# Graph kernel with two attention layers on one core: layer 0's logit projections as four row strips instead of narrow columns, and a smaller, split load ahead of them

## The chip, the cores and the metric

The kernel runs on one core of one Trainium2 chip. The metric is device time in microseconds (us), the median of several executions. TensorE (PE) multiplies matrices, and its weight loads are listed apart as PEld; VectorE (DVE), ScalarE (ACT) and GpSimd (POOL) do the rest; SyncE (SP), ScalarE and GpSimd issue the DMAs. Each engine takes its own instructions in the order in which the program gives them.

## The reference, cut to what matters

`x` is 2708 x 256 and `adj` is 2708 x 2708, nearly all of it zeros. Two layers follow one another, each with a residual and a row-wise norm:

```python
# layer 0, three heads; adj without its diagonal is A
for W, a in heads:                       # W: 256 x 256, a: 512 x 1
    hW = x @ W
    hp = (A > 0) @ hW
    hm = (A < 0) @ hW                    # zero here: no entry of adj is negative
    e  = leaky_relu(concat([hp, hm], axis=1) @ a)
    # softmax over the neighbours with logits e[j], times A, times hW; mean over the heads
out0 = diag(adj) * (gru_edge(A @ x, x) + gru_node(mean_of_heads, x))
x = layernorm(x + out0)
# layer 1: a four-head graph attention on the mask adj > 0.5, residual, layernorm
```

Because `hm` is zero, `e` is `(A > 0) @ (x @ (W @ a[:256]))`. So each head needs one vector `W @ a[:256]` of 256 numbers, and then one number for each row of x. For three heads these numbers are called `u`, 2708 x 3. Only the first 256 of the 512 entries of each `a` enter.

## The kernel before, in words

The rows are cut into 22 blocks of 128 (the last has 20), and the columns into six groups: five of 512 (four blocks each) and one of 148.

The first phase passes over the transposed adjacency group by group, two row blocks at a time. For each pair of blocks, SP loads 128 x 2 x 512 floats (512 KB) into one of five buffers. ACT turns them into 0/1 masks with two Sign passes (into rings of three, `over` and `mask`). DVE takes a maximum over stretches of 64 columns (`found0`). PE then adds the masks up in four matmuls, each on its own 32 columns of the array, that is, on its own 32 rows of a PSUM bank (`only`, `only`, and `u3` twice). The weights `u3` of the last two are the numbers `u` of these row blocks, split into three bf16 parts.

During the first group, each four blocks also load a part of x transposed (`xT`, 256 x 512) and compute their `u` with `projected_u`. It takes three steps:

- `uw`, the three vectors `W @ a[:256]`, is made once by DVE, in six products with a sum along the row (`scalar_tensor_tensor` with `accum_out`). It needs all of `gat_w` (768 KB) and of `a_b` (`a` on all partitions, 768 KB), which ACT's queue loads with one DMA each.
- For each row block, and for both halves of the 256 features, a matmul takes 128 columns of `xT` as weights and streams the three columns of `uw` through them.
- DVE copies the 128 x 12 results out of PSUM and splits them into three bf16 parts (`split3`).

PE has further work without a due time there: 60 `keep` products (the GRU's terms in x for five groups), whose results ACT and DVE copy out of PSUM by turns and SP writes to DRAM.

When the maxima of a group are complete, `listed` and `spread` make lists of the rows that have entries in each stretch of columns. From these lists POOL gathers adjacency rows and table rows with indirect DMAs. The second phase multiplies them for layer 0 and runs the two GRU cells by group; the third does the same for layer 1.

No order is written by hand. Every instruction is noted first (class `Plan`), with a cost from a small model: a float32 matmul costs at least 0.22 or 0.26 us, a transpose 0.11, a DMA 2.5 us and its size at 250 GB/s. A list scheduler then issues, on each engine, the ready instruction with the longest tail behind it. Matmuls into one bank that are noted in a row are issued as one. So each cost that changes can change the order of everything after it. All notes carry line 219 of the profile, where the scheduler calls them, and lines are therefore told apart by the names of tiles. `f_home` stands for several tiles that share one allocation (`uw`, `u3`, `f_u`, the masks and three of the five adjacency buffers among them); the other two buffers are `f_edge_wi` and `f_node_wi`. `side` is a ring of two PSUM banks.

Of the kernel before, what the change touches and what calls it, by code (L numbers as in the profile page):

```python
# [10 lines left out]
F32 = mybir.dt.float32  # L11
# [9 lines left out]
P = 128  # L21
D = 256
KD = D // P
HEADS0 = 3
# [6 lines left out]
CH = 512  # L31
# [277 lines left out]
def fast_path(ctx: ExitStack, tc: tile.TileContext, i: dict, out: bass.AP, bad: bass.AP):  # L309
# [11 lines left out]
    nc = plan = Plan(tc.nc)  # L321
# [6 lines left out]
    GR = CH // P  # L328
    groups = [list(range(g, min(g + GR, NB))) for g in range(0, NB, GR)]
    NG = len(groups)  # L330
    base = [g[0] * P for g in groups]
    width = [sum(size[c] for c in g) for g in groups]
# [20 lines left out]
    def ring(tiles):  # L353

        return cycle(tiles).__next__
# [4 lines left out]
    def banks(name, n):  # L360
        return [ps.tile([P, CH], F32, name=f"{name}{k}") for k in range(n)]
# [3 lines left out]
    side, pl_bank, ls_bank = ring(banks("side", 2)), ring(banks("pl", 1)), ring(banks("ls", 1))  # L365
# [19 lines left out]
    ident = const.tile([P, P], F32, name="f_ident")  # L385
# [32 lines left out]
    QUARTER = P // 4  # L418
# [33 lines left out]
    for t, of in ((less_room, TILES0 + TILES1), (less_whole, WHOLE0 + WHOLE1)):  # L452
        c = 0
        while c < len(of):
            e = c
# [3 lines left out]
            c = e  # L459
# [41 lines left out]
    def on_every(src, wide):  # L501
        return bass.AP(tensor=src.tensor, offset=src.offset, ap=[[0, P], [1, wide]])

    def row_bcast(pool, src, wide, name, queue):
        t = pool.tile([P, wide], F32, name=name)
        queue.dma_start(t, on_every(src, wide))
        return t


    def split3(pool, parts, v, p, n, name):  # L510

        rest = pool.tile([P, n], F32, name=name)[:p]
        if len(v.shape) == 3:
            rest = rest.rearrange("p (b h) -> p b h", h=v.shape[2])
        nc.vector.tensor_copy(parts[0], v)
        nc.vector.tensor_sub(rest, v, parts[0])
        nc.vector.tensor_copy(parts[1], rest)
        nc.vector.tensor_sub(rest, rest, parts[1])
        nc.vector.tensor_copy(parts[2], rest)

    xT = const.tile([P, KD, N], F32, name="f_xT")
# [6 lines left out]
    gat_w = const.tile([P, HEADS0, KD, D], F32, name="f_gat_w")  # L528
# [172 lines left out]
    ap, tiles = Rings(const, 1, home2), Rings(const, 8, home1)  # L701
# [1 line left out]
    nc.vector.memset(u3, 0.0)  # L703
    e_col = const.tile([P, NB, HEADS0], F32, name="f_e_col")
    nc.gpsimd.memset(e_col, 0.0)
    nc.scalar.dma_start(gat_w, i["L0_gnn_gat_W"].rearrange("h (k p) e -> p h k e", p=P))
    a_b = row_bcast(ap, i["L0_gnn_gat_a"], HEADS0 * 2 * D, "f_a_b", nc.scalar)

    uw = ap.tile([P, KD, HEADS0], F32, name="f_uw")
    junk = ap.tile([P, D], F32, name="f_junk")  # L710
    for h in range(HEADS0):
        for k in range(KD):
            nc.vector.scalar_tensor_tensor(
                junk, gat_w[:, h, k, :], 1.0, a_b[:, 2 * h * D : (2 * h + 1) * D],
                op0=ALU.mult, op1=ALU.mult, accum_out=uw[:, k, h : h + 1],
            )

# [4 lines left out]
    def projected_u(g):  # L722
        bl = groups[g]
        n = len(bl) * HEADS0
        pu = side()
        for m, b in enumerate(bl):
            for k in range(KD):
                nc.tensor.matmul(
                    pu[: size[b], m * HEADS0 : (m + 1) * HEADS0], lhsT=xT[:, k, b * P : b * P + size[b]],
                    rhs=uw[:, k, :], start=(k == 0), stop=(k == KD - 1),  # L730
                )
        u = ap.tile([P, GR * HEADS0], F32, name="f_u", bufs=2)
        full = sum(size[b] == P for b in bl) * HEADS0
        if full:
            nc.vector.tensor_copy(u[:, :full], pu[:, :full])
        if full < n:
            nc.vector.memset(u[:, full:n], 0.0)
            nc.vector.tensor_copy(u[: size[last], full:n], pu[: size[last], full:n])
        split3(
            ap, [u3[:, bl[0] : bl[-1] + 1, s * HEADS0 : (s + 1) * HEADS0] for s in range(3)],  # L740
            u[:, :n].rearrange("p (b h) -> p b h", h=HEADS0), P, n, f"f_u_rest{len(bl)}",
        )
# [31 lines left out]
    for b in range(0, NB, 7):  # L774
        e = min((b + 7) * P, N)
# [106 lines left out]
    for g, cs in enumerate(groups):  # L882
        w = width[g]
        sums_of = (accs[0], dbs[0])[g % 2]
        c0, nf = base[g] // W0, w // W0
        for b0 in range(0, NB, 2):
# [4 lines left out]
            for b in pair:  # L891
                if g == 0 and b % GR == 0:
                    load_xT(b // GR)
                    projected_u(b // GR)
# [17 lines left out]
            for b in pair:  # L912
                if b in cs:
                    p, o = size[b], b * P - base[g]
                    v = at2[:p, b - b0, o : o + p]
# [16 lines left out]
            for q, (lhs, rhs) in enumerate(  # L932
# [3 lines left out]
                p = size[pair[q % 2]]  # L936
                nc.tensor.matmul(
                    sums_of[q * QUARTER : (q + 1) * QUARTER, :w], lhsT=lhs[:p], rhs=rhs[:p],
                    start=(b0 == 0), stop=(b0 + 2 == NB),
# [358 lines left out]
    for h in range(HEADS1):  # L1298
        for k in range(KD):
            nc.tensor.matmul(  # L1300
                pm[:C1, h : h + 1], lhsT=w1[:, k, h * C1 : (h + 1) * C1], rhs=xmean[:, k : k + 1],
                start=(k == 0), stop=(k == KD - 1), skip_group_check=True,
# [124 lines left out]
def tile_adj_resnorm(tc: tile.TileContext, i: dict, out: bass.AP):  # L1427
    nc = tc.nc
    with tc.tile_pool(name="guard", bufs=1) as gp:
        bad = gp.tile([P, 1], F32, name="bad")  # L1430
        fast_path(tc, i, out, bad)
        with tc.tile_pool(name="guard_ps", bufs=1, space=PSUM) as ps:
            one = gp.tile([P, 1], F32, name="guard_ones")
            nc.vector.memset(one, 1.0)
            nc.vector.tensor_scalar(bad, bad, 0.0, None, op0=ALU.is_gt)
            n = ps.tile([1, 1], F32, name="n_bad")
            nc.tensor.matmul(n, lhsT=bad, rhs=one, start=True, stop=True)
            flag = gp.tile([1, 1], I32, name="flag")
            nc.vector.tensor_copy(flag, n)
        taken = nc.values_load(flag[0:1, 0:1], min_val=0, max_val=P)  # L1440
        with tc.If(taken > 0):
            general_path(tc, i, out)
# [436 lines left out]
```

## Time and profile before

| | |
|---|---|
| median of 3 runs | 847.95 us (843.71 to 849.48) |
| the profiled execution | 842.26 us, its span 840.3 us |
| PE busy | 732.8 us, 87% of the span |
| DVE / ACT / POOL busy | 614.0 / 546.7 / 526.0 us |
| moved by DMA | 138.71 MB |
| the u matmuls (`side<-f_home,f_xT`) | 88 records in all, 13.1 to 51.4 us |

In the lines of the timeline the columns are: start in us, length in us, engine, line, operation, tile written and tiles read, shapes, how many records are merged, and in brackets the idle time before with what ended it. A float32 matmul of the program leaves two records. "issue" is idle time for which the profile shows no cause.

### The profile page before, as it was taken

To read this page: it belongs to the slowest core of one execution; us is meant where nothing else is said; L and a number is where in the kernel's file an instruction comes from. 1 tells how busy PE (TensorE), PEld (TensorE's weight loads), DVE (VectorE), ACT (ScalarE), POOL (GpSimd) and SP (SyncE) were. 2 spreads that over 40 slices of the span, in tenths; PEclk is the share of its full clock that TensorE was granted. 3 is DMA by queue.
4 is the path that set the end of the run, shared out by engine and by line. 5 is a ranking of instruction groups with operands and counts; after the bars stand their busy time and mean duration, and the time that the engine had idled before them with its cause. 6 is when DMAs were issued, how large, how long until landed. Compare 5 with 4: busy or idle time off the path is not lost.

```text
span 840.3 us, 14025 instructions
## 1 busy us (share of the span) xinstructions
PE 732.8 (87%) x3911; PEld 477.7 (57%) x3911; DVE 614.0 (73%) x2062; ACT 546.7 (65%) x1560; POOL 526.0 (63%) x593
## 2 busy tenths in 40 slices
PE   3978887889889999998998998999998799988871
PEld 3533333334547775676466745745744597877761
DVE  5548677866864646796599748748839689999982
ACT  3569996886557985788386836935943332238796
POOL 3002778787867775577757777777776453777620
PEclk9968999898999999999998999999999799999995
DMA  9578889789974441564255436337424254556521
GB/s 342 182 223 255 265 268 282 232 251 268 259 197 136 117 141 42 166 194 117 66 160 153 102 105 211 99 76 205 127 67 126 68 153 111 170 181 205 143 89 50
DMA packets 88503, 138.71 MB, mean 165 GB/s; under 512 B 21904, under 2 KB 44264, under 8 KB 87776
## 3 DMA queue, kind: packets, MB, share of 16 engines
q1 hardware_dynamic: 67168, 90.56, 33.3%
q0 software_dynamic: 20320, 45.59, 21.9%
q10 hardware_dynamic: 928, 1.57, 0.5%
q8 instruction: 33, 0.54, 0.3%
q14 instruction: 54, 0.44, 0.2%
HBM read 116.18 MB, written 24.26 MB: 167 GB/s over the span
## 4 chain that ended last, share of the span: by engine, by line
PE 20%; DVE 17%; ACT 9%; DMA 4%; issue 3%; POOL 0%; SPq 0%; DVEq 0%; ACTq 0%
PE side L219 13%; DVE f_home L219 12%; PE acc L219 5%; DMA raw<-in_adj_dram,f_idx 3%; ACT y L219 2%; ACT f_home L219 2%; PE db L219 2%; ACT four L219 2%; DVE f_xn L219 1%; ACT f_xn L219 1%; DMA rows<-f_T,f_idx 1%; DVE ids L219 1%; ACT L219 1%; DVE four L219 1%; PE pl L219 0%
## 5 line engine op out<-in xcount | busy, mean ns | idle before, releaser
L219 POOL DMA_INDIRECT rows<-f_T,f_idx x254 | 252.4, 994 | 124.2 <-ACT four L219 32.1
L219 PE MATMUL acc<-four,rows 128*128 128x256 f32 (+1 forms) x712 | 180.0, 389 | 8.6 <-ACT four L219 3.8
L219 ACT ACTIVATE four<-four,rows 128x64 f32<-128x64 f32 (+1 forms) x534 | 144.4, 336 | 25.8 <-DVE four L219 11.1
L219 PEld LDWEIGHTS acc<-four,rows 128*128 128x128 f32 x712 | 129.0, 191 | 38.8 <-issue 13.0
L219 POOL DMA_INDIRECT raw<-in_adj_dram,f_idx x91 | 90.4, 994 | 37.3 <-issue 14.5
L219 POOL DMA_INDIRECT f_home<-in_adjT_dram,f_idx x67 | 68.5, 1022 | 19.8 <-issue 15.0
L219 POOL DMA_INDIRECT f_xn<-in_adjT_dram,f_idx x63 | 63.7, 1011 | 18.3 <-issue 16.7
L219 PE MATMUL acc<-f_home,rows 128*65 128x128 f32 (+2 forms) x512 | 66.8, 282 | 6.8 <-DVE f_home L219 4.4
L219 PEld LDWEIGHTS acc<-f_home,rows 128*65 128x65 f32 (+1 forms) x512 | 56.6, 141 | 12.9 <-DVE f_home L219 7.1
L219 PE MATMUL side<-f_home,f_node_wi 128*128 128x512 f32 (+1 forms) x144 | 59.7, 547 | 1.7 <-DVE f_home L219 1.7
L219 PE MATMUL side<-f_home,f_edge_wi 128*128 128x512 f32 (+1 forms) x144 | 57.3, 544 | 0.0
L219 PE MATMUL side<-f_home,f_gat_w 128*128 128x512 f32 (+1 forms) x144 | 55.6, 542 | 1.2 <-DVE f_home L219 1.2
L219 DVE SCALAR_TENSOR_TENSOR f_home<-pl,rows,f_m 128x128 f32<-128x128 f32 x196 | 55.8, 341 | 0.1
L219 DVE TENSOR_TENSOR f_home<-f_home,side 128x512 f32<-128x512 f32 (+1 forms) x64 | 42.0, 659 | 17.6 <-PE side L219 16.0
L219 PE MATMUL db<-f_home,rows 128*65 128x128 f32 x376 | 50.4, 288 | 4.9 <-DVE f_home L219 2.5
L219 ACT ACTIVATE f_home<-f_home,f_minus_half 128x1024 bf16<-128x1024 f32 (+5 forms) x44 | 42.0, 966 | 15.0 <-issue 7.4
L219 DVE TENSOR_REDUCE f_found<-f_home 128x16 f32<-128x1024 f32 (+8 forms) x52 | 43.8, 863 | 8.0 <-POOL f_home L219 7.3
L219 ACT ACTIVATE f_m<-four 128x64 bf16<-128x64 f32 (+1 forms) x181 | 40.7, 246 | 12.3 <-DVE four L219 10.3
L219 DVE SCALAR_TENSOR_TENSOR f_home<-ls,rows,f_m 128x128 f32<-128x128 f32 (+1 forms) x168 | 46.5, 337 | 2.0 <-ACT ls L219 1.1
L219 PEld LDWEIGHTS db<-f_home,rows 128*65 128x65 f32 x376 | 41.3, 142 | 11.7 <-DVE f_home L219 4.1
L219 POOL DMA_INDIRECT f_m<-in_adjT_dram,f_idx x33 | 33.1, 1003 | 22.8 <-DVE f_rel L219 13.3
L219 DVE TENSOR_SCALAR f_m<-raw 128x128 uint8<-128x128 f32 (+1 forms) x91 | 20.8, 241 | 34.8 <-DMA raw<-in_adj_dram,f_idx 34.6
(234 smaller groups left out, 1523.0 us busy)
## 6 DMA issues: line engine op xcount, KB each, us to landing
f_home<-in_adjT_dram SPq DMA_DIRECT2D x30, 512.0 KB
f_XH<-kept SPq DMA_DIRECT2D x60, 256.0 KB
f_home<-f_XH SPq DMA_DIRECT2D x60, 256.0 KB
f_node_wi<-in_adjT_dram SPq DMA_DIRECT2D x10, 512.0 KB
f_edge_wi<-in_adjT_dram SPq DMA_DIRECT2D x10, 512.0 KB
f_home<-f_TS SPq DMA_DIRECT2D x5, 1024.0 KB
rows<-f_T SPq DMA_DIRECT2D x33, 132.0 KB
rows<-f_T,f_idx POOLq DMA_INDIRECT x254
```

Source lines behind the costliest of these rows:

```text
L219: call = lambda: f(*args, **kwargs)
```

## The change

It has two parts.

The loads: of each attention vector only the first 256 entries are put on all partitions (384 KB instead of 768 KB). This DMA goes first on ACT's queue, and `gat_w` follows with one DMA for each head (256 KB each). DVE's products for a head need only that head.

The projection, for groups of 512 rows: `uw` is padded with zeros to 32 columns and becomes the weight, and `xT` streams. Four matmuls cover the two feature halves and the two halves of the 512 rows; each writes to its own 32 rows of a PSUM bank, 256 columns wide. ACT copies the 128 x 256 result to SBUF, PE turns it with two 128 x 128 transposes into the other `side` bank, and DVE copies one feature half and adds the other. `split3` is as before, now in a function of its own. The last group (148 rows) keeps the old way.

```diff
-    nc.scalar.dma_start(gat_w, i["L0_gnn_gat_W"].rearrange("h (k p) e -> p h k e", p=P))
-    a_b = row_bcast(ap, i["L0_gnn_gat_a"], HEADS0 * 2 * D, "f_a_b", nc.scalar)
-
-    uw = ap.tile([P, KD, HEADS0], F32, name="f_uw")
+    a_b = ap.tile([P, HEADS0, D], F32, name="f_a_b")
+    gat_a = i["L0_gnn_gat_a"]
+    nc.scalar.dma_start(
+        a_b, bass.AP(tensor=gat_a.tensor, offset=gat_a.offset, ap=[[0, P], [2 * D, HEADS0], [1, D]])
+    )
+    for h in range(HEADS0):
+        nc.scalar.dma_start(gat_w[:, h], i["L0_gnn_gat_W"][h].rearrange("(k p) e -> p k e", p=P))
+
+    uw = ap.tile([P, KD, QUARTER], F32, name="f_uw")
+    nc.vector.memset(uw, 0.0)
...
-                junk, gat_w[:, h, k, :], 1.0, a_b[:, 2 * h * D : (2 * h + 1) * D],
+                junk, gat_w[:, h, k, :], 1.0, a_b[:, h, :],
...
         pu = side()
+        if width[g] == CH:
+
+            half = CH // 2
+            for q in range(4):
+                k, c0 = q % KD, base[g] + q // KD * half
+                nc.tensor.matmul(
+                    pu[q * QUARTER : (q + 1) * QUARTER, :half], lhsT=uw[:, k, :], rhs=xT[:, k, c0 : c0 + half],
+                    start=True, stop=True,
+                )
+            by_row = ap.tile([P, half], F32, name="u_rows", bufs=2)
+            nc.scalar.copy(by_row, pu[:, :half])
+            pt = side()
+            for j in range(half // P):
+                nc.tensor.transpose(pt[:, j * P : (j + 1) * P], by_row[:, j * P : (j + 1) * P], ident)
+            halves = pt[:, :half].rearrange("p (j f k c) -> p k f j c", j=half // P, f=2, k=KD)
+            u = ap.tile([P, GR * HEADS0], F32, name="f_u", bufs=2)
+            v = u.rearrange("p (f j h) -> p f j h", f=2, h=HEADS0)
+            nc.vector.tensor_copy(v, halves[:, 0, :, :, :HEADS0])
+            nc.vector.tensor_add(v, v, halves[:, 1, :, :, :HEADS0])
+            split_u(g, u)
+            return
```

More of the change, by code (lines that the diff above doesn't have):

```diff
@@ L502, in on_every @@
         return bass.AP(tensor=src.tensor, offset=src.offset, ap=[[0, P], [1, wide]])
[L504 to L507, printed above, removed]
     def split3(pool, parts, v, p, n, name):
@@ L729, in projected_u @@
                     pu[: size[b], m * HEADS0 : (m + 1) * HEADS0], lhsT=xT[:, k, b * P : b * P + size[b]],
-                    rhs=uw[:, k, :], start=(k == 0), stop=(k == KD - 1),
+                    rhs=uw[:, k, :HEADS0], start=(k == 0), stop=(k == KD - 1),
                 )
@@ L738, in projected_u, with split_u @@
             nc.vector.tensor_copy(u[: size[last], full:n], pu[: size[last], full:n])
+        split_u(g, u)
+    def split_u(g, u):
+        bl = groups[g]
+        n = len(bl) * HEADS0
         split3(
```

## The prediction

> **What bounds the kernel now.** I read the page's row of slices first, then the timeline of each engine over the first 60 us, where everything lies that the diff touches, then the waits of POOL, to see whether time won there reaches the end.
>
> ```profile
> PE   3978887889889999998998998999998799988871
> ...
> ACT  3569996886557985788386836935943332238796
> ...
> DMA  9578889789974441564255436337424254556521
> ```
>
> A slice is 21 us. PE is the fullest engine nearly everywhere, except in the first slice. DMA is at nine tenths in the first slice and at five in the second: the loads start at full rate and then starve. The windows give this in figures.
>
> ```profile
> 8.00:20.20 12.20, 7.12 (x34) 7.01 (x34) 7.28 (x22) 7.46 (x7) 2.06 (x4) 1.00 1.04 389
> 20.20:31.00 10.80, 9.92 (x54) 7.55 (x53) 5.04 (x21) 4.08 (x4) 0.00 (x0) 1.00 0.91 313
> 31.00:46.00 15.00, 12.28 (x49) 6.30 (x46) 9.27 (x16) 11.57 (x14) 0.00 (x0) 0.94 0.43 116
> ```
>
> The columns are the stretch, its length, busy time of PE, PEld, DVE, ACT and POOL, then clock, DMA share and GB/s. The rate falls from 389 to 116 GB/s: a load needs a free adjacency buffer, and buffers come free through ACT and DVE. The timelines say what these waited for.
>
> ```profile
> 10.50 0.43 DVE L219 SCALAR_TENSOR_TENSOR f_home<-f_gat_w,f_home 128x256 f32<-128x256 f32 x1 [5.09 <-DMA f_home<-in_L_gnn_gat_a_dram]
> ```
>
> ```profile
> 13.07 7.16 PE L219 MATMUL side<-f_home,f_xT 128*128 128x3 f32 x32 [13.07 <-DVE f_home L219]
> 20.16 0.61 PE L219 MATMUL acc<-f_home,f_only 128*32 128x512 bf16 x2
> ...
> 23.05 6.99 PE L219 MATMUL side<-f_home,f_xT 128*128 128x3 f32 x32
> ...
> 30.94 3.45 PE L219 MATMUL acc<-f_xT,f_edge_wh 128*128 128x512 f32 x4
> 34.23 1.88 PE L219 MATMUL db<-f_xT,f_edge_wh 128*128 128x512 f32 x4
> ...
> 41.35 1.95 PE L219 MATMUL side<-f_home,f_xT 128*128 128x3 f32 x16
> ```
>
> ```profile
> 21.29 1.15 ACT L219 ACTIVATE f_home<-f_node_wi,f_minus_half 128x1024 bf16<-128x1024 f32 x1 [3.95 <-issue]
> ...
> 34.43 0.59 ACT L219 COPY kept<-acc 128x512 f32<-128x512 f32 x1 [9.06 <-PE acc L219]
> ```
>
> So the first group hangs on a chain. The a and gat_w loads land at 10.5; six DVE products last until 13.6; PE then does u for two groups in 7.2 us, and for two more from 23.05 to 30.04; only then come the keep product and the copy for which ACT sat idle 9.06 us (3.95 us before that it waited for a mask buffer, which PE's mask matmuls free). PE itself is the bottleneck here, at little useful work.
>
> Whether this counts at the end is shown by POOL's waits from 78 to 232 us.
>
> ```profile
> POOL f_xn L219 <- issue: 16.7, 57, 0.3
> POOL f_m L219 <- DVE f_rel L219: 13.3, 1, 13.3
> POOL f_m L219 <- issue: 9.5, 32, 0.3
> ```
>
> POOL waits 13.3 us once, for the first list of the first group (first gather at 78.55), and then gathers without a pause beyond 0.3 us each. PE is busy 189 of 200 us between 420 and 620. Neither has slack that would swallow a later start; so an earlier end of the first group should mostly reach the end.
>
> [...] the two keep products above, alike in shape, take 3.45 and 1.88 us, and the change falls at 34.2, 3.3 us after dense work began. The u matmuls (0.22 us a record at 13 us, 0.12 at 41) never brought it about. The clock row shows full speed there, so durations are to be believed, not that row. [...] four mask matmuls start at 39.47 and the next four at 39.70. For float32 no row shows it. [...] ACT's 1.57 MB landed by 10.4 us at 0.197 MB/us, half of 389 GB/s; agrees.
>
> **The change, part by part.**
>
> *The loads.* ACT's queue carries 1.18 MB instead of 1.57. Transfers begin at about 2.4 us; at 0.197 MB/us the last head lands at 2.4 + 6.0 = 8.4 instead of 10.4. Two further issues of about 0.5 us on ACT's queue lie in ACT's idle time until 9.74. Four of six DVE products then hide under the loads and two remain, 2 x 0.53 = 1.1 us instead of 3.1. DVE is idle from 5.4 to 10.5, so the memset of uw is free. uw is ready at 9.5 instead of 13.6, and u starts about 3.6 us earlier. The 0.39 MB less also bring later loads forward by 1 us.
>
> *The projection.* For each of five groups 16 records go: 3.55 us cold (7.16 / 2), 1.95 warm. Eight records of 256 float32 columns come, each half of a keep record: 0.43 us cold, 0.22 warm. If the quarters ran fully side by side they would take two records, 0.86 us cold; one after another, eight, 3.45. [...] So I take that the second record of a quarter overlaps only with the first of the next: five records, 2.15 us cold. Then ACT's copy of 128 x 256: between the cast of 128 x 32 (0.19) and the copy of 128 x 512 (0.57) it is 0.37. Two transposes, 0.27 each where the trace has such, 0.55 together. One more DVE operation, 0.17. Moves without a wait make 2.15 + 0.37 + 0.55 and two hand-overs of 0.1, that is 3.27 us for a group, against 3.55: in the cold state the matmuls themselves gain almost nothing in length.
>
> *The added wait.* The transposes wait for ACT, and ACT has Sign passes of 1.04 to 1.15 us in its queue. Behind the waiting transposes stand PE's mask matmuls and keep products; behind those ACT's own mask buffers. Moreover each group now takes both side banks, so the next group's matmuls cannot begin before ACT has copied; before, two groups ran ahead. The wait is at least 0 and I take 0.6 us, half a Sign; a bad place in ACT's order means a pair of Signs, 2.2 us, or a Sign that itself waits for a mask buffer, 3 us and more.
>
> *The sum.* uw at 9.5; u of group 0 on PE to 11.8, copied at 12.4, turned at 13.0, split at 14.6 to 15.2 (17.9 before); group 1 on PE until 16.4 and split at 18.3 (22.4 before). That frees the mask buffers earlier and shortens ACT's wait of 3.95. Groups 2 and 3 end on PE at about 25.3 (30.04), keep begins there, still cold, and ACT's copy comes at 28.8 instead of 34.4: 5.6 us. The last full group is off the chain after that. Of these some is lost to buffers that are not yet filled; PE's cold and warm stretches move by chance as well. I take 5.3 us at the end of the first group and 0.85 of it at the end of the kernel, an estimate from the slackless POOL and PE: 4.5 us.
>
> The scheduler's costs change too: it sees 1.72 us instead of 2.08 for a group's matmuls, plus a copy and two transposes, and smaller loads. The order of later work can shift; nothing in the trace prices that, and I bound it by 5 us both ways, with 0 taken.
>
> The profiled execution's 842.26 us, 2.0 above its span, becomes 837.8. The median of the runs lies 5.7 above it; the same 4.5 off the median gives 843.5 us.
>
> **The rivals.**
>
> *Faster by over 1%.* If the quarters run fully side by side, 1.3 us a group over four groups is 5.2 more; or the steady streams of 256 columns warm the clock early, and the keep product costs 1.9 instead of 3.45. Then 5.3 + 5.2, or more, times 0.85, 9 to 12 us: about 837. For it speaks the bf16 packing; against it, the weight loads between the two float32 passes.
>
> *Hidden anyway.* ACT's backlog takes the place of PE's: 22 Sign passes of 1.1 us for the first group are 24 us whatever PE does, and DVE's eleven maxima of 1.2 us hold buffers too. Or a new order eats it. Gain 0 to 2: about 847. For it speaks that ACT runs without a gap from 34.4 to 46.5.
>
> *Slower.* The hand-over to ACT in the first group. With no packing a group costs 3.45 + 0.37 + 0.55 + 0.2 = 4.57 us plus the wait. At 3 us of wait, four groups lose 4 x (7.57 - 3.55) = 16, less 4.6 from the loads, 11.5; times 0.85, plus 10: about 858. It decides (over 8.5 us at the end) from a mean wait of 2.6 us without packing, 3.9 with my five records. Against it: the scheduler puts the copy early, since all of the first group's masks hang on it.
>
> **How the numbers follow.** Forecast (some 4.5 us less) 0.44, faster rival 0.24, hidden 0.16, slower rival 0.16. About 1% is what a measurement of this kernel tells from no change: under 839.5 counts as faster, over 856.4 as slower. Both middle cases fall within. So faster 0.25, same 0.58, slower 0.17. The range reaches into both outer cases, 836 to 857; the likeliest case alone, with the order's 5 us, is 838 to 849.
>
> **What would show it.** Right: first DVE product at under 7 us and the last at 9 to 10; u matmuls as 8 records a group; first mask matmul near 16 instead of 20.16; ACT's idle time before its first kept copy down from 9 us to 3; first gather at about 73 instead of 78.55, and the end as much earlier. Wrong: four quarters in 0.9 us cold (too timid), PE idle for over 2 us ahead of the transposes on ACT (slower rival), or a first gather that is earlier while the end is not (order).

## The result, and the profile after

The kernel after takes 834.23 us (median of 4 runs, 831.39 to 834.91) against 846.31 us of the kernel before beside it (4 runs, 843.71 to 849.48). The ratio is 0.987, 95% interval 0.9843 to 0.9897: about 11 us less. The forecast was 843.5 with a range from 836; it lies too high, and the change is worth more than twice what was taken for it. The profiled execution took 833.86 us with a span of 832.0, 8.4 us less than that of before. The profile of before (842.26) lay below its four runs, so the two profiles show some 3 us less than the ratio does.

The row of slices of the kernel after:

```profile
PE   2798787889899899999997998999998899998871
...
ACT  4869979786469884795487736836843422247796
...
DMA  9867888779974441654453545436424344556521
```

The second slice of the DMA row is where the first group was short of loads: it stood at 5 and is now at 8. The windows of the same three stretches (columns as before):

```profile
8.00:20.20 12.20, 5.18 (x36) 1.74 (x38) 8.20 (x28) 8.23 (x10) 2.09 (x4) 1.00 1.06 384
20.20:31.00 10.80, 9.09 (x45) 3.69 (x38) 7.54 (x21) 7.89 (x10) 0.00 (x0) 1.00 0.83 308
31.00:46.00 15.00, 10.49 (x50) 4.18 (x49) 9.58 (x28) 14.72 (x19) 0.00 (x0) 0.80 0.88 278
```

From 31 to 46 us the loads run at 278 GB/s instead of 116, and ACT is busy for 14.72 of 15 us: from there on the bound of the first group is ACT and no longer PE. In the first stretch PE is busy for 5.18 of 12.2 us instead of 7.12. DVE's timeline shows the products that make `uw`:

```profile
9.02 0.43 DVE L219 SCALAR_TENSOR_TENSOR f_home<-f_gat_w,f_home 128x256 f32<-128x256 f32 x1 [3.61 <-DMA f_gat_w<-in_L_gnn_gat_W_dram]
...
11.10 0.45 DVE L219 SCALAR_TENSOR_TENSOR f_home<-f_gat_w,f_home 128x256 f32<-128x256 f32 x1 [1.18 <-DMA f_gat_w<-in_L_gnn_gat_W_dram]
11.89 1.22 DVE L219 TENSOR_REDUCE f_found<-f_home 128x16 f32<-128x1024 f32 x1 [0.34 <-POOL f_home L219]
...
13.96 0.42 DVE L219 SCALAR_TENSOR_TENSOR f_home<-f_gat_w,f_home 128x256 f32<-128x256 f32 x1
```

The first product comes 1.5 us earlier than before, but the last ends at 14.4, later than before. The second head lands only at 11.1, and the scheduler has put a maximum of 1.22 us between the products. PE's timeline:

```profile
13.98 1.54 PE L219 MATMUL side<-f_xT,f_home 128*32 128x256 f32 x8 [13.98 <-DVE f_home L219]
16.00 1.08 PE L219 MATMUL side<-f_xT,f_home 128*32 128x256 f32 x8 [0.48 <-ACT f_home L219]
17.01 0.69 PE L219 MATMUL side<-f_ident,f_home 128*128 128x128 f32 x2
...
19.73 0.64 PE L219 MATMUL acc<-f_home,f_only 128*32 128x512 bf16 x2
...
24.02 0.39 PE L219 MATMUL acc<-f_home,f_only 128*32 128x512 bf16 x2 [1.15 <-ACT f_home L219]
...
25.78 1.88 PE L219 MATMUL acc<-f_xT,f_edge_wh 128*128 128x512 f32 x4
```

So u starts 0.9 us later than before. But a group then costs 1.5 us (the first) or 1.1 us, not 3.55, and all four groups still run at half clock. "Full clock" and "half clock" (warm and cold) are names for two lengths of equal work: keep products of before took 1.88 and 3.45 us, eight records of the new projection take 0.64 (at 36.68) and 1.08 us. The traces show these lengths; the clock column of the windows stands at 1.00 from 8 to 31 us in both kernels, so that a clock is behind them is my reading. The keep product starts at 25.78 instead of 30.94, and it already runs at full clock (1.88, not 3.45). ACT's first kept copy follows at 27.70 instead of 34.43:

```profile
27.70 0.59 ACT L219 COPY kept<-acc 128x512 f32<-128x512 f32 x1 [2.53 <-PE acc L219]
```

And POOL's first gather comes 7.9 us earlier (it was at 78.55), after a wait as long as ever:

```profile
70.68 1.15 POOL L219 DMA_INDIRECT f_m<-in_adjT_dram,f_idx  x1 [13.58 <-DVE f_rel L219]
```

The next group ends keep this lead: the flags (`f_least`) of the second to the fourth group come at 83.29, 113.09 and 151.94, against 91.16, 120.95 and 159.81 before, each 7.9 us earlier. At the flags of the fifth group it is 6.0 us (189.70 against 195.69), and at the first gather of table rows, where the second phase begins, 5.1. In a second pair of profiles, described below, it is 7.1 to 7.3 us at all of these places.

### The profile page after: what moved, and what is told of

It is laid out like the page before. It is cut to its first block, busy times and chain, and to the rows that moved or that the text cites. A ratio compares the mean times of both kernels' runs of the same rounds, so it can differ in the third digit from the quotient of the medians.

```text
span 832.0 us, 13985 instructions
## 1 busy us (share of the span) xinstructions
PE 723.2 (87%) x3881; PEld 466.5 (56%) x3881; DVE 614.2 (74%) x2068; ACT 547.6 (66%) x1565; POOL 530.3 (64%) x593
## 4 chain that ended last, share of the span: by engine, by line
PE 22%; DVE 15%; ACT 8%; DMA 6%; issue 3%; POOL 1%; DVEq 0%; SPq 0%; ACTq 0%; POOLq 0%
PE side L219 13%; DVE f_home L219 10%; PE acc L219 5%; DMA rows<-f_T,f_idx 3%; DMA raw<-in_adj_dram,f_idx 3%; PE db L219 2%; ACT y L219 2%; ACT f_home L219 2%; ACT four L219 1%; DVE f_xn L219 1%; ACT f_xn L219 1%; DVE four L219 1%; ACT L219 1%; DVE ids L219 1%; POOL raw L219 1%
## 5 line engine op out<-in xcount | busy, mean ns | idle before, releaser
L219 POOL DMA_INDIRECT rows<-f_T,f_idx x254 | 253.1, 996 | 120.3 <-PE acc L219 24.9
L219 POOL DMA_INDIRECT f_home<-in_adjT_dram,f_idx x67 | 69.6, 1038 | 19.8 <-issue 13.3
L219 POOL DMA_INDIRECT f_xn<-in_adjT_dram,f_idx x63 | 65.8, 1044 | 18.3 <-issue 16.2
L219 DVE TENSOR_TENSOR f_home<-f_home,side 128x512 f32<-128x512 f32 (+2 forms) x69 | 42.6, 621 | 15.7 <-PE side L219 15.0
L219 ACT ACTIVATE f_home<-f_home,f_minus_half 128x1024 bf16<-128x1024 f32 (+5 forms) x44 | 42.3, 967 | 12.2 <-PE db L219 5.0
```

The source lines that it names most:

```text
L219: call = lambda: f(*args, **kwargs)
```

## The experiments

The first four ran on a chip on which the kernel before itself took 996.62 us, 18% more than elsewhere; the difference arises after some 80 us. Its cause is open: with the loads alone the gathers last as long there (0.99 us on average, against 1.01 elsewhere), but POOL stands idle ahead of them for 354 us in all, not 221. Of these runs I use the first 80 us, and ratios.

### The loads alone and the projection alone

The loads alone: the new DMAs in the kernel before.

```diff
-                junk, gat_w[:, h, k, :], 1.0, a_b[:, 2 * h * D : (2 * h + 1) * D],
+                junk, gat_w[:, h, k, :], 1.0, a_b[:, h, :],
```

> The kernel before with only the new loads (first 256 entries of each vector, weights by head); u is still made by matmuls of three columns. Theory (the gain is the time that PE needs for u: quarters side by side, and the clock that they warm early): 0 to 2 us less than before, about 845, because in the changed kernel the last DVE product still ended at 14.4 us, and ACT's transfers got a third of the bandwidth and not half. First gather at 77 to 79 us. Rival 'the loads, and the order of loads they bring about, carry the gain': 6 to 11 us less, about 837, first gather near 72. Rival 'the order of the schedule': anything between, with a first gather that does not explain the end.

Ratio 0.9974 (0.9937 to 1.001), first gather at 75.41. The projection alone is the kernel after with the two DMAs of before.

> The changed kernel with the loads of before (all 512 entries, one DMA for the weights): only the projection by rows. Theory (PE's time for u): 8 to 11 us less than before, 835 to 838; four quarters in about 1.0 us cold, full clock near 24 us, first gather at 70 to 73 us. Rival 'the loads carry it': 0 to 4 us less, 842 to 846, first gather at 75 or later.

Ratio 0.9963 (0.9932 to 0.9994), first gather at 71.31, that is, nearly the 70.68 of the kernel after. But on this chip the projection brought 0.4%, some 4 us, and not the 8 to 11 us of its theory. As the whole time could not separate the two parts, both were run again on an ordinary chip.

> The kernel before with the smaller loads alone. Theory A (the loads bring nothing, because the new queue packets are served at a third of the traffic and the first product of u is no earlier): 843 to 847 us, first gather 77 to 78.6, first flags about 58. Theory B (the loads carry a share of the gain): 838 to 841, first gather 74 to 76. POOL's wait of 3 to 5 us for ACT's kept rows near 250 us stays under A.

842.95 us, ratio 0.9972 (0.9957 to 0.9988): 2.4 us less, at the edge of theory A. First gather at 77.50, first flags at 57.62, as theory A said; POOL's wait near 250 us, which it expected to stay, is gone. In the kernel with the loads alone, PE shows what they did:

```profile
13.96 7.03 PE L219 MATMUL side<-f_home,f_xT 128*128 128x3 f32 x32 [13.96 <-DVE f_home L219]
22.85 6.99 PE L219 MATMUL side<-f_home,f_xT 128*128 128x3 f32 x32
30.74 3.78 PE L219 MATMUL acc<-f_xT,f_edge_wh 128*128 128x512 f32 x4
```

u starts 0.9 us later than before and the keep product as late as before. So up to the keep product the loads bring nothing. What the 2.4 us are is taken up below, with the order of work.

> The kernel after with the loads of before, so the projection by quarters alone. Theory A (the projection carries all of the gain): 832 to 837 us, first gather 70.5 to 71.5, no wait of POOL for kept rows near 250 us. Theory B (both parts needed): 838 to 841.

834.22 us, ratio 0.9872 (0.9817 to 0.9927), first gather at 71.15. Theory A holds: the projection alone, with the order of work that comes with it, gives what both parts give together.

### How much is "side by side"

The kernel after, with the four quarter products made over all 128 columns, the weights padded with zeros, and added up in one bank. Nothing else differs but the small copies that lay out these weights.

```diff
-                    pu[q * QUARTER : (q + 1) * QUARTER, :half], lhsT=uw[:, k, :], rhs=xT[:, k, c0 : c0 + half],
-                    start=True, stop=True,
+                    pu[:, :half], lhsT=uw4[:, q, :], rhs=xT[:, k, c0 : c0 + half],
+                    start=(q == 0), stop=(q == 3),
```

> The changed kernel with the four products of a group each made by weights of 128 columns, zero outside their own 32, added up in one bank: the same 128 x 256 result, the same copy and transposes, but nothing side by side. Theory (packing is most of the gain): eight records one after another, 3.45 us a group cold instead of 1.0, so 2.4 us more for each of the first two or three groups and some 5 us more at the end, 838 to 840. Rival 'the clock': a dense stream of 3.45 us warms the clock even earlier, before 20 us, and later groups then take 1.7 us; loss of 1 to 2 us only, 835 to 836. If packing does not matter at all: 834.

Ratio 0.9964 (0.9933 to 0.9996), first gather at 73.25. Again on an ordinary chip:

> The kernel after, with the four quarter products replaced by four products over all 128 columns (weights padded with zeros), accumulated in one bank: it takes away only that the quarters run side by side. If running side by side is worth what the first gathers showed: first gather 72.5 to 73.5 instead of 70.8, total 835 to 838 us. If it decides the order of work later as well: 840 or more. If it is worth nothing: 834.

837.67 us, ratio 0.9917 (0.989 to 0.9943), first gather at 73.35: 3.4 us more than the projection by quarters in the same batch, of which 2.2 show at the first gather. PE's timeline of this kernel tells the most:

```profile
14.75 3.78 PE L219 MATMUL side<-f_xT,f_home 128*128 128x256 f32 x8 [14.75 <-DVE f_home L219]
19.00 1.99 PE L219 MATMUL side<-f_xT,f_home 128*128 128x256 f32 x8 [0.46 <-ACT f_home L219]
...
29.43 1.88 PE L219 MATMUL acc<-f_xT,f_edge_wh 128*128 128x512 f32 x4
```

Without quarters side by side, the first group costs 3.78 us, as much as the 3.55 of before. The second costs 1.99, which is also what the narrow products cost at full clock (1.95, at 41.35 in the profile before). So at either clock a group costs PE what it cost before. Yet this kernel is 7.5 us faster than before, and 5.3 us faster than the kernel with the loads alone, whose order of work it shares. What differs on PE is the clock: it doubled between the first group (3.78 us) and the second (1.99), and the four groups take 9.65 us in all instead of 14.15. In the kernel after they take 4.78 us, all of it at half clock.

### Does any early work on PE raise the clock?

The kernel before, with 32 matmuls of 484 columns of zeros on PE before everything else.

```diff
+    warm = pl_bank()
+    for _ in range(32):
+        nc.tensor.matmul(
+            warm[:, : NB * NB], lhsT=ones_h, rhs=flags1.rearrange("p a b -> p (a b)"), start=True, stop=True
+        )
```

> The kernel before with 32 matmuls of 484 bf16 zeros ahead of its first work on PE, into a bank that nothing else uses until later; they change no result. Theory part 'the clock': PE reaches full speed by about 8 us instead of 34; the u matmuls of the first four groups take 1.8 to 2 us a group instead of 3.55, the first keep 1.9 instead of 3.45: 5 to 8 us less, 838 to 841. If the clock is not part of the gain, or falls back before 13 us: 845 to 848. If the added matmuls stay cold they end after 16 us and cost up to 3 us: 849.

```profile
3.18 7.99 PE L219 MATMUL pl<-f_flags,f_ones_h 128*128 128x484 bf16 x32 [3.18 <-POOL f_flags L219]
13.58 0.38 PE L219 MATMUL side<-f_home,f_xT 128*128 128x3 f32 x2 [2.42 <-DVE f_home L219]
14.18 4.86 PE L219 MATMUL side<-f_home,f_xT 128*128 128x3 f32 x30 [0.21 <-DVE f_home L219]
...
22.13 6.99 PE L219 MATMUL side<-f_home,f_xT 128*128 128x3 f32 x32
...
30.03 3.51 PE L219 MATMUL acc<-f_xT,f_edge_wh 128*128 128x512 f32 x4
```

Of the 32 records of the first two groups 30 take 4.86 us, where all 32 took 7.16 before, so the clock was up when they began. But it did not stay: in the trace their distance goes from 0.11 to 0.21 us at 16.1, the next two groups take 6.99 again, and the keep product 3.51. First gather at 77.73, ratio 1.0017 (0.9987 to 1.0047): no gain. PE was "busy" here for 7 us at a stretch, and the clock stayed at half. Products of three columns did not raise the clock here (6.99 us, and the keep product after them 3.51), and those of 256 columns in the unpacked kernel did (1.99 us after 3.78). Whether the narrow products also let it fall, or the 2.42 us without work ahead of them, was not separated.

### The hand-over to ACT, and the loads once more

The kernel after and the kernel before once more show the scatter.

> The changed kernel once more, as the yardstick on the chip of the next runs. Theory: 10 to 12 us less than before; full clock near 24 us, first gather at 70 to 72 us.

833.67 us, ratio 0.9872 (0.9828 to 0.9915). First gather at 70.83. Here the keep product at 25.91 was cold (3.48 us; mask products at 24.05 had already run at full clock, 0.40 us instead of 0.64) and ACT's kept copy came at 29.43, but the flags of the first group came at 51.15 against 50.50. So in the kernel after it hardly matters whether the clock turns just before or just after the first keep product: the two first gathers differ by 0.15 us.

> The kernel before, with a profile on the same chip. Theory (the first group, and then nothing): its first gather 7 to 9 us later than the changed kernel's, and every later mark of the first phase as much later. Rival 'part of the gain arises later': the distance grows to 11 or 12 us at the end.

844.86 us, ratio 0.9996 (0.997 to 1.0021), first gather at 78.06.

In the next kernel DVE, not ACT, takes the 128 x 256 result out of PSUM:

```diff
-            nc.scalar.copy(by_row, pu[:, :half])
+            nc.vector.tensor_copy(by_row, pu[:, :half])
```

> The changed kernel with the copy of the 128 x 256 result by DVE instead of ACT: the hand-over to ACT is gone. Theory (the hand-over to ACT costs little, since the copies waited 0.3 to 2 us): within 2 us of the changed kernel, either side. Rival 'the hand-over is the price of the change': 3 us or more less than the changed kernel.

833.5 us, ratio 0.9872 (0.9835 to 0.9908). The hand-over to ACT, which my slower rival rested on, costs nothing that can be seen.

Then the loads of the kernel after on SP's queue instead of ACT's:

```diff
-        nc.scalar.dma_start(gat_w[:, h], i["L0_gnn_gat_W"][h].rearrange("(k p) e -> p k e", p=P))
+        nc.sync.dma_start(gat_w[:, h], i["L0_gnn_gat_W"][h].rearrange("(k p) e -> p k e", p=P))
```

(and `a_b` likewise).

> The changed kernel with the loads of the vectors and weights on SP's queue instead of ACT's; the scheduler then puts them ahead of everything but x's first part. Theory (on ACT's queue these loads in 1 KB pieces got a third of the bandwidth, and the products of DVE ended at 14.4 us for that reason and because a maximum was put between them): alone on the queue they land by about 7 us, the products end by 8 to 9, u starts about 5 us earlier; ACT and the loads of the adjacency come next, so 2 to 4 us less than the changed kernel. Rival 'the start is not the bound any more, ACT's Sign passes are': within 1 us of the changed kernel.

834.13 us, ratio 0.9884 (0.9851 to 0.9916), no gain over the kernel after:

```profile
10.79 1.28 ACT L219 ACT_TABLE_LOAD   x1 [10.79 <-DMA f_home<-in_adjT_dram]
9.94 1.54 PE L219 MATMUL side<-f_xT,f_home 128*32 128x256 f32 x8 [9.94 <-DVE f_home L219]
...
25.64 3.62 PE L219 MATMUL acc<-f_xT,f_edge_wh 128*128 128x512 f32 x4
```

u starts 4 us earlier, as I had wanted of the loads. The keep product starts at the same time: 25.64 against 25.78. Ahead of it in PE's order stand mask matmuls, and these wait for ACT's Sign passes, as the line at 24.02 of the kernel after shows (1.15 us idle, released by ACT, though the last packet of the keep product's `f_edge_wh` had landed at 21.56). In the kernel after ACT's ten Sign passes for the first five pairs of blocks run from 9.58 to 24.9 with 4.1 us of idle time, 2.5 of them in wait for the result of u. The trial is not clean, though. On SP's queue these loads stand ahead of the adjacency, whose first block now lands at 10.79 instead of 8.29; ACT's ten passes run from 12.09 to 24.1 with 0.95 us of idle time. So ACT is the bound here, and "hidden anyway" is right for this way of bringing the loads forward. What an earlier u without that delay would bring was not tried; ACT's idle time puts it at some 2.5 us at most, by estimate.

### The order of work

In these profiles the lead is 7 to 8 us up to the fourth group, and 5.1 us (7.1 in the second pair) at the first row gather. It grows again at the change from the first phase to the second: from the first row gather to the first product with `gat_w` the kernel before takes 87.6 us (88.8 in the second profile), the kernel after 83.3 (83.9). In the kernel before, POOL stands still there once:

```profile
250.45 1.50 POOL L219 DMA_INDIRECT rows<-f_T,f_idx  x1 [4.65 <-ACT kept L219]
```

This is from the second profile of before; the first has 3.29 us at the same place. In the kernel with the loads alone the corresponding gather does not wait:

```profile
245.81 0.94 POOL L219 DMA_INDIRECT rows<-f_T,f_idx  x1 [0.30 <-ACT kept L219]
```

To see what order alone does, I changed only one number of the scheduler's model in the kernel before, no instruction:

```diff
-                t = max(0.22 if rows <= C1 + 1 else 0.26, n / 595)
+                t = 0.1 if n == 3 and ins[0].tensor.name.startswith("f_xT") else max(0.22 if rows <= 65 else 0.26, n / 595)
```

> The kernel before, with no instruction changed; only the planner's assumed cost of a product of u is lowered from 0.26 to 0.1 us, so that its order of instructions becomes another. Theory A (a part of the gain is only the other order at the change from the first phase to the second): first gather stays at 77.5 to 79, POOL's wait for kept rows near 250 us goes, the stretch from the first row gather to the first product with gat_w shrinks from 88 to about 84, total 839 to 842 us. Rival (the order alone is worth nothing, or the wait stays): 843 to 847.

842.21 us, ratio 0.9959 (0.9939 to 0.9978): 3.5 us from order alone. But not where theory A had it: the first gather came at 76.49, the first row gather at 227.22 (230.79 before), and the stretch at the change of phases grew to 89.1. The wait for kept rows was gone, and others had come. So the total comes within 0.3 us of theory A's range, and its mechanism does not hold.

The same with 0.4 in place of 0.1:

> The kernel before, no instruction changed; the planner's assumed cost of a product of u is raised from 0.26 to 0.4 us, a third order of the same work. Theory A: first gather 76 to 81, the stretch at the change of phases in 83 to 89, total within 4 us of 844.5. Theory B: the stretch is 86.5 to 89 as in the other orders of the old projection.

851.33 us, ratio 1.0083 (1.0046 to 1.0119): 7 us slower, where theory A allowed 4; the stretch, 88.7, fits both theories. Its first gather is at 64.45, the earliest of all; so the first gather tells of the end only between kernels of like order. Likewise in the kernel after, with the cost of a quarter product taken as 0.26 instead of 0.43:

> The kernel after, no instruction changed; only the planner's assumed cost of a quarter product is lowered from 0.43 to 0.26 us, so that its order becomes another. It shows how much an order drawn anew moves the time. Theory A (order is worth a few us either way): first gather 68 to 73, the stretch from the first row gather to the first product with gat_w anywhere in 82 to 89, total 831 to 840. Theory B (the stretch of 83 to 84 us belongs to the new projection whatever the order): 83 to 84.5 and 832 to 836.

836.08 us, ratio 0.9903 (0.9871 to 0.9935), first gather at 78.06, the stretch 84.1. The stretch fits theory B, the first gather neither.

Last, the kernel after with its order kept and the first group made late: four unpacked products, made twice, of which the scheduler counts one pass.

```diff
-            for q in range(4):
+            for q in list(range(4)) * 2:
...
+                nc.free = nc.free or q == 3
+            nc.free = False
```

(`free` makes the scheduler's cost 0.)

> The kernel after with its own order of work, but each group's four products taken over all 128 columns and made twice (the second pass writes the same numbers and counts nothing in the planner), so that PE spends about 4 to 7 us a group on u, as the kernel before did or more. First gather about 77 to 79, as before. Theory A (the gain of 10 us is the 7 us of the first group and, apart from it, some 3 us of another order at the change from the first phase to the second): that second part stays, the stretch from the first row gather to the first product with gat_w is 83 to 84.5 us, total 840 to 843. Theory B (all of the gain comes from the first group's earlier end, and the later 3 us follow from it): the stretch is 86.5 to 89 again, total 844 to 847.

```profile
14.68 5.25 PE L221 MATMUL side<-f_xT,f_home 128*128 128x256 f32 x16 [14.68 <-DVE f_home L221]
20.39 3.72 PE L221 MATMUL side<-f_xT,f_home 128*128 128x256 f32 x16 [0.46 <-ACT f_home L221]
...
34.47 1.88 PE L221 MATMUL acc<-f_xT,f_edge_wh 128*128 128x512 f32 x4
```

First gather at 79.73, 9.05 us later than after. 844.91 us, ratio 1.0009 (0.9982 to 1.0035). The stretch is 84.1, as theory A said, but the total is that of theory B. So with the first group as late as before (in fact 1.2 to 1.7 us later), the gain of 11 us is gone, within 2 us. POOL's gathers stand in the same order here as in the kernel after, and they stay 8.7 to 11.0 us late to the end; the two spans, 841.7 and 832.0, differ by 9.7. So in this order all of a delay of the first group reaches the end.

What the order gave by itself is best read from the kernel with the loads alone. Counted from the profiles, 180 of PE's 3,911 records stand elsewhere in it than in the kernel before. Between it and the kernel after, apart from the projection itself, only four of PE's, three of ACT's, some 17 of DVE's, two of SP's and none of POOL's do. So it has nearly the order of the kernel after, with u as late as before, and it gains 2.4 us (1.0 to 3.6); the loads' own share of that was not separated. Its stretch is 86.3 us, and so seems to speak against the order as the cause. But 1.9 us of it are one fall of the clock after a wait, as two lines of 12 equal records show:

```profile
273.08 4.75 PE L219 MATMUL acc<-four,rows 128*128 128x256 f32 x12 [1.74 <-ACT four L219]
277.76 2.84 PE L219 MATMUL acc<-four,rows 128*128 128x256 f32 x12
```

The stretch is no sure mark of one order either: after_order, in another order, has 84.1 as well. What makes it shorter stays open.

Four kernels of one batch make a ladder. The last three share nearly all of their order:

| kernel | median, us | less than the line above | first gather |
|---|---|---|---|
| before | 845.19 | | 78.55, 78.06 (other batches) |
| loads alone | 842.95 | 2.2 | 77.50 |
| u by rows, one product after another (`unpacked_2`) | 837.67 | 5.3 | 73.35 |
| u by rows, four side by side (`proj_only_2`, loads of before) | 834.22 | 3.4 | 71.15 |

By the intervals of their ratios to before, the last three are known to 1.3, 2.2 and 4.6 us either way. The projection thus gives some 8.7 us of 11, and loads and order the rest. Of the 8.7 the first gathers show 6.4 to 6.8.

## Why the prediction was wrong, point by point

The direction was right, and so was the place; the size was less than half. The three terms of the sum, 5.3 us at the first group, times 0.85, plus 0 for the order, were each too small: the runs give 7.2 to 7.9, about 1, and about 2.4 (with the loads' share). The step whose mechanism was wrong is the cost of a group: five records in a row, 2.15 us, so that the matmuls "gain almost nothing in length". Measured are 1.1 us at half clock, because all four quarters run side by side. The faster rival (chance 0.24, "about 837") had the mechanism: the quarters side by side. Its other half, an early full clock, carries the kernel without quarters, and adds little beside them.

| step of the sum | predicted | measured in the kernel after |
|---|---|---|
| last product of `uw` ends, u starts | 9.5 | 14.4, 13.98 |
| matmuls of one group, cold | 2.15 us | 1.1 us (first group 1.5) |
| ACT's copy, two transposes | 0.37, 0.55 us | 0.37, 0.69 us |
| first keep product starts | 25.3, cold | 25.78, at full clock (25.91, cold, in the second profile) |
| ACT's first kept copy | 28.8 | 27.70 (29.43 in the second profile) |
| first gather | about 73 | 70.68 (70.83) |
| share that reaches the end | 0.85 | about 1 (9.7 of 9.05 us in after_held) |
| effect of order | 0, bound 5 | about 2.4, with the loads |

*The loads: wrong.* "At 0.197 MB/us the last head lands at 8.4" assumed that ACT's queue gets half of the traffic. The second head landed 2.08 us after the first (11.10 and 9.02), with 0.262 MB: 0.126 MB/us, a third of 384 GB/s. The queue lines of the two profiles, before and then after, with packets and MB:

```profile
q10 hardware_dynamic: 928, 1.57, 0.5%
```

```profile
q10 hardware_dynamic: 1216, 1.18, 0.4%
```

The change removed the large packets (`a_b` in rows of 6 KB, now 1 KB); the mean packet fell from 1.7 KB to 0.97 KB, beside SP's rows of 2 KB. From 7 to 12 us the trace of the kernel after has 661 packets on ACT's queue and 659 on SP's, nearly all of 1 and of 2 KB, which gave ACT's queue 0.64 of 1.90 MB, a third. In the kernel before, from 7 to 9 us, when `a_b` came in its large packets, it has 115 and 110, and ACT's queue moved 0.31 MB/us. The counts are not equal everywhere: from 4 to 6 us of the kernel before they are 540 and 120. I had reckoned with equal bytes for both queues, and taken 0.197, a mean over both sizes of packet and a slow start (ACT's first packet comes at 2.89 us), for a steady half. That the size of the packets sets the share was not shown: a kernel that changes it alone was not run. I had also not reckoned with the scheduler placing a maximum between the products. By the estimate from ACT's idle time, at most some 2.5 us of this error of 4.5 could have reached the sum; ACT's Sign passes would have hidden the rest.

*The quarters: the step that failed.* I took it that only neighbours overlap, five records; nothing in the trace of before showed that for float32. The 1.1 us are little more than the two records (0.86) that the fully parallel case gives: in the second group of the kernel after four records start at 16.00 to 16.02 us and the other four at 16.43 to 16.45, and the group takes 1.08 us cold against 3.78 one after another. The weight loads, which I had set against the faster rival, last 0.20 us there for all eight (PEld at 16.00).

*The clock: a miss, but one that cost little.* I wrote that the u matmuls "never brought it about" and still kept the first keep product cold after the change. In the unpacked kernel streams of 256 columns doubled the clock some 4 us after they began (begun at 14.75, 1.99 us for the group at 19.00). In the kernels with narrow products 7 us of three-column products at a stretch did not raise it (7.16 us, then 6.99, in the kernel before). In the kernel after, the clock turned only at 22 to 24 us (the group at 21.79 still took 1.08 us, the mask products at 24.02 took 0.39 where they had taken 0.64), when the four groups of u were over or nearly so. With the first keep product cold (3.48 us in the second profile) the first gather still came at 70.83. So the 5.3 us of the unpacked kernel, which PE's timeline puts down to the clock, are not a part of the gain of the kernel after that could be added to the quarters: they are what the clock gives where the quarters are missing.

*The two errors partly cancelled.* u started 4.5 us later than I had it, and was some 1.1 us a group shorter. So that the keep product came at 25.78, almost the predicted 25.3, was luck: it stood behind mask matmuls that waited for ACT. The rival's 10.5 us at the first group became 7.2 to 7.9 for this reason too: ACT's Sign passes were the next bound. From ACT's first kept copy (6.7 us earlier, 5.8 in the second pair) to the first gather the lead grew by 1.1 to 1.5 us, where I had it shrink by 0.3; what added this was not taken apart.

*The pass-through: too low.* I took 0.85 "from the slackless POOL and PE". In after_held a delay of 9.05 us at the first gather is one of 9.7 us in the span. In the first pair of profiles the lead wavers on the way, from 7.9 to 5.1 and up again.

*The order: drawn by luck.* Three runs with no instruction changed moved the total by -3.5, +7 and +2 us. One lies outside the bound of 5 us, and 0 was as good a middle as any; for the kernel after the draw was favourable.

*The slower rival* is refuted by the time itself, and its hand-over to ACT by the kernel with DVE's copy. *Hidden anyway* fits the loads only, as far as they were tried.

With the measured terms the sum reads: 6.8 us at the first gather (77.50 to 70.68, in nearly one order) times 9.7/9.05, plus 2.4. The prediction would have been some 9.7 us below the median shown, 838. Against the 11 us measured (8.7 to 13.3 by the interval of the ratio) that leaves 1.3 us, within the scatter.

## What to carry to other kernels

Small products that fill only 32 columns of the array may be worth laying side by side in float32 too: here that took a group from 3.55 to 1.1 us. Ask of a matmul not only how long it takes but whether its shape raises the clock: here streams of 256 columns did (3.78 us for the first group, 1.99 for the second), products of three columns behind 128-column weights didn't (7.16 us for two groups, then 6.99), though PE was busy through these stretches. When the engine at the bound becomes shorter, name the next engine in the chain (here ACT's Sign passes) before crediting any earlier start. Where a list scheduler draws the order, run a variant that changes only its costs, to know how much of a difference of a few microseconds is order.

## What the runs showed of the hardware that was not expected

- Four float32 matmuls on four column strips of 32 ran side by side: 8 records of 256 columns took 1.08 us cold and 0.64 us warm, against 3.78 and 1.99 one after another.
- A clock that was already up fell again under narrow products, after 2.42 us without work: 30 records of 3 columns in 4.86 us (part of them at full clock), then 32 in 6.99 us, all at half.
- A wait of 1.74 us in the midst of dense work was followed by half clock: 12 records in 4.75 us, then 12 equal ones in 2.84.
- The moment at which the clock turns varies between executions: the same keep product at 25.8 us took 1.88 us in one profile of the kernel after and 3.48 in the other, and the total hardly differed.
- In two stretches two busy queues were served about equal numbers of packets, not of bytes: 115, most of them of 6 KB, beside 110, most of 2 KB, moved 0.31 MB/us on ACT's queue (7 to 9 us of the kernel before), and 661, most of 1 KB, beside 659, most of 2 KB, only 0.13 (7 to 12 us of the kernel after). From 4 to 6 us of the kernel before it was 540 beside 120.
- One chip ran the kernels 18 to 19% slower, from about 80 us on. The first gather agreed with the other chips for two kernels (71.31 and 71.15, 73.25 and 73.35), and came 2.1 us earlier for the third.
